# Row sums from one accumulated tensor, the normalisation on GpSimd, and matmul operands at one byte modulo 512

## The chip, the cores and the metric

The kernel runs on one core of a Trainium2 chip. A core has a matrix engine (TensorE, PE in the profile; its weight loads are listed apart as PEld), a vector engine (VectorE, DVE), a scalar engine (ScalarE, ACT), GpSimd (POOL), and a sync engine (SP) whose queue here issues nearly all transfers. Each engine works through its own instructions in the order in which they were written down and waits on semaphores for the others. Operands lie in on-chip memory (SBUF, 128 partitions), matmul results in eight banks of an accumulation memory (PSUM).

The metric is the device time of one execution in microseconds (us). A kernel is executed several times; one execution is also taken with the hardware profiler, and the profile's "span" runs from its first to its last instruction.

## What is computed

One transformer block on `x` of shape (2, 1024, 512) in float32: adaptive layer norm, causal attention with 32 query heads and 8 key/value heads of width 64, output projection with a gate, a second adaptive norm, and a feed-forward part with ternary weights. Cut to what matters here:

```python
q = apply_rope((x @ Wq).reshape(b, s, H, D).transpose(0, 2, 1, 3), pos)
k = apply_rope((x @ Wk).reshape(b, s, KVH, D).transpose(0, 2, 1, 3), pos)
v = (x @ Wv).reshape(b, s, KVH, D).transpose(0, 2, 1, 3)
scores = jnp.einsum('bhqd,bhkd->bhqk', q, k) / jnp.sqrt(jnp.float32(D))   # k, v repeated for 4 query heads each
scores = jnp.where(causal[None, None], scores, jnp.finfo(x.dtype).min)
attn = jax.nn.softmax(scores, axis=-1)
out = jnp.einsum('bhqk,bhkd->bhqd', attn, v)
x = x + ga * (out @ Wo)
h = _layernorm(x) * (1 + cb) + sb
gate, up = jnp.split(h @ ternary_quant(w_gate_up).T, 2, axis=-1)
x = x + gb * (rms_norm(silu(gate) * up) @ ternary_quant(w_proj).T)
```

The softmax's denominator is a sum over keys of the exponentials; the kernel computes it apart from the product with `v` and divides at the end.

## The kernel before

**Precision.** Most matmuls are F32R: each operand that needs more than that format holds is split into a high and a low part (names ending in H and L), and two or three products are added up in PSUM. A full F32R matmul has a 128x128 stationary tile and 512 moving columns. The product of exponentials and values (`po`) and the row sums (`pr`) are plain F32 matmuls, which the profile lists as two records each.

**Stages.** Four blocks of 512 tokens go through norm, transposes, keys (`pqk` from `wk`), values (`pv`) and queries (`pqk` from `wq`), with results stored to device memory. Then comes attention (some 300 to 1070 us), the output projection (`pj`, to some 1250 us), and the feed-forward part: hidden products (`pgu`, 16 chunks of 8+8 matmuls for each block of 512 tokens) and the second product (`pfo`, 8 matmuls for each chunk).

**Attention** is cut into 64 units (lines 576 and 755 on): batch, key/value head `g`, and 256 query positions `i`, for the four query heads of the group at once. A unit walks over `nb = 2*i + 2` blocks of 128 keys, so 2, 4, 6 or 8 of them; the last group walks `i` backwards. For each unit:
- `top_mm` and `top_red` (lines 797 and 805): high parts of queries and keys are multiplied to find each row's maximum (`pm`, reduced by VectorE into `mm` and `mx`), which is turned into a row and later subtracted from the scores by a fourth matmul (`unit` times `row`);
- `score(j)`: 4 pairs of matmuls into two PSUM banks, each pair on the two halves of the array's rows;
- `expo`: ScalarE writes the exponentials of key block j into the tile `e[j]` (128 keys x 4 heads x 256 queries); `causal`: GpSimd's affine_select blanks the upper triangle in the last two blocks;
- `value`: `po` accumulates values times `e[j]`, in steps of SPAN[nb] key blocks; `copy_out` copies it to `on`;
- `total(j, ...)` (line 901): the exponentials are added up into `acc`, half a tile (two heads) an instruction, the last block's in one. Before the change, all blocks but number nb-2 go into `acc`; the first add is `e[0] + e[1]`. VectorE does the adds of block j where `j % VSUM == 1` (with VSUM 9: block 1), and all adds of the last LAST units; GpSimd does the others (lines 942 and 943);
- `row_sum` (line 953): `pr = ones.T @ e[nb-2] + ones.T @ acc`, four matmuls of 256 columns each (one for each head, on a 32-column strip of the array), so eight; with nb = 2 it is `e[0]` and 128 columns of `e[1]`;
- `row_copy`, `row_turn`, `invert`, `put_inv`, `get_inv`: the sums go by three transfers through a narrow tile `l8` (where VectorE inverts them) and device memory (`linv`) and come back broadcast as `ri`; `normalize` (line 993) multiplies `on` by `ri` on VectorE; `keep` stores it.

**Order.** From line 587 on nothing is issued directly: every piece of work is a task with an engine, an estimated cost, a due time, the tasks it waits for and the buffers it takes, and `Plan.run` (line 102) writes them down one by one in the order that its own estimates give. TensorE's choice among ready tasks (line 131) goes by due time, less STICK for a task of the same array tiling as the one before, plus terms that favour tasks feeding VectorE (`feeds`: the maximum matmuls) when VectorE's backlog is under FEED, and disfavour them over ENOUGH. The array tilings are the modes: 0 full, 1 two column halves (`value`), 2 column strips (`row_sum`), 3 two row halves (`score`, `top_mm`). Once built, each engine's order is fixed.

**Buffers.** 6 + 10 tiles for exponentials (tags `e` and `eb`), 2 for `acc`, 4 for `on`, 2 for `ri`. An `e` tile is free again when its `value` and its adds (before the change, for block nb-2, the row sum) are done.

**Pools.** Tiles lie in pools opened and closed as the stages go. A pool starts where the one before it ends, so small tiles decide at which byte the large ones start. Before the change the small tiles `ct`, `st`, `mv`, `ve` and `rs` are in the first pool `lA`, beside the weights `wk` and `wv`, and `ve2`, `rs2` in the feed-forward pool `cC`. The build places the tiles so (start byte modulo 512): `wkH`, `wvH` 192; `wqH`, `hH`, `hL` 480; `t`, `k1`, `k2`, `h2_0`, `h2_1` 192; `vt` 192 and 480; `woH` and `woL` of the first four groups and `oh` 480, of the other groups 192; `gu0` to `gu5` 192, `gu6` onward 480; `mH`, `mL` and `pj0`, `pj1` 192, the other `pj` 320.

Nearly every instruction carries line 39, that of the recording helper, in the profile; tile names tell them apart.

Of the kernel before, what the change touches and what calls it, by code (L numbers as in the profile page):

```python
# [8 lines left out]
F32 = mybir.dt.float32  # L9
# [3 lines left out]
ALU = mybir.AluOpType  # L13
# [4 lines left out]
B, S, E = 2, 1024, 512  # L18
# [4 lines left out]
EC = E // 128  # L23
# [38 lines left out]
class Plan:  # L62
# [10 lines left out]
    def add(self, eng, cost, due, emit, after=(), order=(), takes=(), dma=0, mode=0, lane=None):  # L73
        t = Task(len(self.tasks), eng, cost, due, emit, after, order, takes, dma, int(isinstance(cost, Two)) if eng == "V" else mode, lane)
        self.tasks.append(t)
        return t
# [102 lines left out]
SPAN = {2: 2, 4: 4, 6: 6, 8: 4}  # L179
HELD = 4  # L180
TBEG, TEND, PER_UNIT = 300.0, 20.0, 0.8
VSUM, VSIGN, LAST = 9, 1, 3
TBEFORE, TGAP, TSKIP = 20, 20.0, 25.0
LEAD, SPREAD, STICK, LATE = 11.0, 0.6, 6.0, 2.0
ENTER, LEAVE, LOAD, AHEAD = 0.16, 0.37, 0.1, 0.25
CLASS = (0, 1, 1, 2)
TURN, SPARE = 0.05, 1.0
FEED, BOOST, ENOUGH, DELAY, FILL = 0.6, 12.0, 3.0, 8.0, 2.0
QT, PACE = 6, 4

@with_exitstack
def block_kernel(ctx, tc, x, wq, wk, wv, wo, wgu, wpj, cin, wmod, cos, sin, out):
    nc = tc.nc
    T = InOrder(tc, nc.tensor, True)
    V, A, P, SY = (InOrder(tc, e, False) for e in (nc.vector, nc.scalar, nc.gpsimd, nc.sync))
# [38 lines left out]
    ones = const.tile([128, 32], F32, name="ones")  # L234
# [73 lines left out]
    def pool(stack, name, bufs=1, **kw):  # L308
        return stack.enter_context(tc.tile_pool(name=name, bufs=bufs, reuse_waits="tile", **kw))


    left, right = ExitStack(), ExitStack()
    lp, hp0 = pool(left, "lA"), pool(left, "h0A")
    rp, hp1, tp = pool(right, "wA", side="right"), pool(right, "h1A", side="right"), pool(right, "tA", 2, side="right")

# [5 lines left out]
    cs = rp.tile([128, S], F32, name="cs")  # L321
    sn = rp.tile([128, S], F32, name="sn")

    ct = lp.tile([128, EC, B], F32, name="ct")
    SY.dma_start(ct, cin.rearrange("(k p) b -> p k b", p=128))
    A.activation(sc[:, :, 0:B], ct, AF.Silu)
    V.tensor_tensor(pick, ident[:, 0:B], ident[:, 32:32 + B], ALU.add)
# [64 lines left out]
    def stats(blk, t):  # L392
        d = st_x[blk]
        if t == 0:
            d["st"] = lp.tile([128, 4, 6], F32, name="st")
            d["mv"] = lp.tile([128, 4, 2], F32, name="mv", bufs=2)
        V.bn_stats(d["st"][:, t, :], d["x"][:, t, :])
        V.bn_aggr(d["mv"][:, t, :], d["st"][:, t, :])

    def rstd(blk, a=0, b=4):  # L400
        d = st_x[blk]
        if a == 0:
            d["ve"] = lp.tile([128, 4], F32, name="ve")
            d["rs"] = lp.tile([128, 4], F32, name="rs", bufs=2)
        V.tensor_scalar(d["ve"][:, a:b], d["mv"][:, a:b, 1], 1e-5, None, ALU.add)
        P.tensor_tensor(d["rs"][:, a:b], d["ve"][:, a:b], mhalf[:, a:b], ALU.pow)

# [158 lines left out]
    for blk in range(NT // 512):  # L566
        keys_values(blk)
        if blk < NT // 512 - 1:
            for g in range(KVH):
# [7 lines left out]
    NU = len(units)  # L577
# [11 lines left out]
                     h=2, h2=1, rab=2, rcd=2, rr=2, gs=2, hm=2, mH=2, mL=2, s2=2, sq=2, y=2, sm2=1))  # L589

    def pe(n):
        return n / 2400 + 0.018

    def dv(n):
        return 0.069 + n / 960

    def dd(n):
        return Two(dv(n))

    def po(n):  # L600
        return 0.2 + n * 0.00205
# [5 lines left out]
    add = plan.add  # L607
# [4 lines left out]
    for g in range(KVH):  # L612
        d, due = {}, 5.2 * g
# [121 lines left out]
    for u, (b, g, i) in enumerate(units):  # L735
        nb = 2 * i + 2
        for j in range(nb):
            due_s[(u, j)] = t
            n = 128 if j == nb - 1 else 256
# [12 lines left out]
    late_e = {key: n % (EB + EL) >= EB for n, key in enumerate((u, j) for u, (b, g, i) in enumerate(units) for j in range(2 * i + 2))}  # L752
    early = [key for key in late_e if not late_e[key]][:EB]

    def attention(u):
        b, g, i = units[u]
        d = U[u]
        nb = 2 * i + 2
        t0, t1_ = due_s[(u, 0)], due_s[(u, nb)]
        prev = U[u - 1] if u else None  # L760

# [7 lines left out]
        if u % NI == 0:  # L769
# [13 lines left out]
            for n in range(4):  # L783
                kd["l"].append(add("S", 0.46, t0 - 26 + n, lambda n=n: load_k(n), order=kd["l"] + (held or before),
                                   takes=(("k1",), (), ("k2",), ())[n], dma=256 * KB))
# [44 lines left out]
        for s in range(2):  # L830
            n = 2 * i + s + 1
# [4 lines left out]
        for n, (h0, s_, c, lo, hi) in enumerate(jobs):  # L836
# [3 lines left out]
            tag = "mx" if hi == 2 * i + s_ + 1 else "mm"  # L840
            for n_, h in enumerate((h0, h0 + 2)):
                r = add("V", dv(w) + ((0.075 if c else 0.015) if tag == "mx" else 0.0), due + 0.01 * n_, lambda a=(h, s_, c, lo, hi): top_red(*a), (m,), order=[low[h, s_]] if c else (),
                        takes=() if tag in seen else (tag,))
# [19 lines left out]
        def score(j):  # L863
            q0 = 128 if j == nb - 1 else 0
            for hp_ in range(2):
                d["p", j, hp_] = stile("ps_").rearrange("p (b q) -> p b q", q=256)
            for n in range(4):
                for hp_ in range(2):
                    r = slice(hp_ * 64, hp_ * 64 + 64)
                    w_, x_ = ((kd["k", 0], d["t"][r, 0]), (kd["k", 0], d["t"][r, 1]), (kd["k", 1], d["t"][r, 0]), (unit, rows[u % 2][r]))[n]  # L870
                    w_ = w_[r] if n == 3 else w_[r, j * 128:(j + 1) * 128]
                    T.matmul(d["p", j, hp_][:, :, q0:], w_, x_[:, :, q0:], start=(n == 0), stop=(n == 3))
# [35 lines left out]
        ex, es, vals, sums = {}, {}, [], []  # L908
        adds, later = {}, []
        for j in range(nb):  # L910
            n = 128 if j == nb - 1 else 256
            due = due_s[(u, j)]
            es[j] = []
            p = add("T", 4 * pe(2 * n) + 0.03, due, lambda j=j: score(j), d["lq"] + kd["l"] + [row] + (cleared[1:2] if u == 0 else []),
                    takes=("#", "#1"), mode=3)
            if late_e[u, j] or (u, j) not in early:
                p.order(opened)
            kd["use"].append(p)
            d.setdefault("sc", []).append(p)
            for hp_ in range(2):  # L920
                x_ = add("A", ac(2 * n), due + 0.5 + 0.5 * hp_, lambda j=j, h=hp_: expo(j, h), (p,), order=es[j],
                         takes=() if hp_ else ("eb",) if late_e[u, j] else ("e",))
                if late_e[u, j]:
                    x_.order(opened)
                p.hold(("#", "#1")[hp_], x_)
                es[j].append(x_)
            ex[j] = es[j]
            if j >= nb - 2:
                ex[j] = [add("P", 0.6, due - 1, lambda j=j: causal(j), es[j])]
            if (j + 1) % SPAN[nb] == 0:  # L930
                js = range(j + 1 - SPAN[nb], j + 1)
                v = add("T", (SPAN[nb] * 2048 - (1024 if j == nb - 1 else 0)) / 2400 + 0.02, due + 5,
                        lambda js=js: [value(x) for x in js], sum((ex[x] for x in js), []) + [kd["lv"]], order=vals[-1:],
                        takes=("#",) if j == SPAN[nb] - 1 else (), mode=1)
                kd["av"].append(v)
                vals.append(v)
            if nb > 2 and j > 0 and j != nb - 2:
                later.append((j, n, due))
        for j, n, due in later:
            for h in range(0, 4, 2 if n == 256 else 4):  # L940
# [8 lines left out]
        out_ = add("A", ac(512), due_s[(u, nb - 1)] + 5, copy_out, (vals[-1],), order=(opened,), takes=("on",))  # L949
# [2 lines left out]

        def row_sum():
            d["pr"] = xtile([128, 256], "pr")
            for n, (a, q0) in enumerate(((d["e", nb - 2], 0), (d["acc"], 0) if nb > 2 else (d["e", 1], 128))):
                for h in range(4):
                    T.matmul(d["pr"][h * 32:h * 32 + 32, q0:], ones, a[:, h, q0:], start=(n == 0), stop=(n == 1))

        def row_copy():
            d["ls"] = tp.tile([128, 256], F32, name="ls", bufs=1)  # L960
# [14 lines left out]
            for a in range(2):  # L975
                SY.dma_start(d["ri"][a * 64:a * 64 + 64, :], linv[u][a:a + 1, :].broadcast_to([64, 512]))

        rs = add("T", 8 * (256 if nb > 2 else 192) / 2400 + 0.02, t1_ + 4, row_sum, sums[-2:] + ex[nb - 2] + ex[nb - 1], takes=("#",), mode=2)
        d["rs"] = [rs]
        if sums:  # L980
            sums[0].hold("acc", rs)
        for j in range(nb):
            es[j][0].hold("eb" if late_e[u, j] else "e", vals[j // SPAN[nb]], *([rs] if nb == 2 or j == nb - 2 else adds[j or 1]))
        rc = add("A", ac(256), t1_ + 5, row_copy, (rs,), order=(opened,), takes=("ls",))
        rs.hold("#", rc)
        rt = add("S", 0.63, t1_ + 5, row_turn, (rc,), takes=("l8",), dma=16 * KB)
# [4 lines left out]
        gi = add("S", 0.92, t1_ + 8, get_inv, (pi,), takes=("ri",), dma=256 * KB)  # L991

        def normalize():
            V.tensor_tensor(d["on"], d["on"], d["ri"], ALU.mult)

        def keep():
            SY.dma_start(os_[b][g][:, :, i * 256:i * 256 + 256], d["on"].rearrange("p (a q) -> p a q", q=256))

        nm = add("V", dd(512), t1_ + 13, normalize, (gi, out_))
        gi.hold("ri", nm)  # L1000
        kp_ = add("S", 0.46, t1_ + 15, keep, (nm,), dma=256 * KB)
        out_.hold("on", kp_)
# [9 lines left out]
    for u in range(NU):  # L1012
        attention(u)
# [264 lines left out]
    n, count, before = 0, 4 * EC * 2 + FC, TBEFORE  # L1278
# [72 lines left out]
    def feed_forward(blk):  # L1351
        nonlocal prev_h, prev_p, prev_l
        d = Cd[blk]
# [47 lines left out]
        def proj(f, ts=range(4)):  # L1401
            if f == 0:
                d["po"] = [otile("pfo") for _ in range(4)]
            for t in ts:
                for n in range(2):
# [4 lines left out]
                  takes=(home_h(n),), dma=512 * KB) for n in range(2) for c in range(2)]  # L1410
# [4 lines left out]
        for f in range(FC):  # L1415
            if blk == 0:
                load_weights(f)
                if f >= PACE:
# [4 lines left out]
                      takes=("#", "gu")) for o in range(2)]  # L1423
# [24 lines left out]
            if final and f >= FC - 2:  # L1448
                p = [add("T", 2 * pe(512), due + 2 * STEP + 3.4 + 0.4 * t, lambda f=f, t=t: proj(f, (t,)), (mh, ml, lpj[f]), order=prev_p)
                     for t in range(4)]  # L1450
                for t in range(1, 4):
# [7 lines left out]
                    takes=("#", "#1", "#2", "#3", "po") if f == 0 else ())  # L1459
# [17 lines left out]
                T.matmul(d["pm"][:, t:t + 1], d["sq"][:, t * 128:(t + 1) * 128], ones[:, 0:1], start=True, stop=True)  # L1477

        def var2():
            d["ve"] = cp.tile([128, 4], F32, name="ve2", bufs=2)  # L1480
            V.tensor_scalar(d["ve"], d["pm"], 1.0 / HID, F32_EPS, ALU.mult, ALU.add)

        def root2():
            d["rs"] = cp.tile([128, 4], F32, name="rs2", bufs=2)
            P.tensor_tensor(d["rs"], d["ve"], mhalf, ALU.pow)

        def scale_y(t):
# [39 lines left out]
        for t in range(4):  # L1527
            cy.append(add("A", ac(512), due + 0.5 * t, lambda t=t: copy_y(t), (prj[-1],), order=cy[-1:] + list(gate_b_use),
                          takes=("y",) if t % 2 == 0 else ()))
# [51 lines left out]
```

## Time and profile before

| | |
|---|---|
| runs | 1624.47, 1624.91 and 1631.88 us; median 1624.91 |
| profiled execution | 1624.7 us |
| its span | 1622.0 us, 27506 instructions |
| mean granted TensorE clock | 0.994 of full |
| TensorE matmul busy | 1579.7 us, 97% of the span |
| VectorE busy | 1192.8 us, 74% |
| GpSimd busy | 763.3 us, 47% |
| ScalarE busy | 694.2 us, 43% |
| transfers | 239.58 MB, mean 148 GB/s |

A busy time is the union of an engine's instructions. Matmuls overlap in their pipeline, so a full F32R matmul lasts 390 to 400 ns by itself while one starts every 230 ns or so; the distance from start to start, or the length of a run of them divided by their number, is what counts. A row of the costliest groups names the tile written and the tiles read, the shapes, the number of instructions, busy time and mean length, and then the engine's idle time just before them with what ended most of it.

### The profile page before, as it was taken

The numbers are of one execution on the slowest core, as the hardware profiler recorded it, in microseconds if no ns is written. First come the engines' busy times: TensorE is split into PE (matmuls) and PEld (weight loads), VectorE is DVE, ScalarE is ACT, GpSimd is POOL, SyncE is SP. The second block draws the span as 40 slices with busy tenths as digits, with TensorE's granted clock in tenths as the row PEclk, the third lists the DMA queues.
The fourth block names the chain that finished last, engine by engine and source line by source line (L and its number), as shares of the span: only waits on it lengthen the run. The fifth ranks groups of instructions, "written<-read, shape, count | busy, mean of one in ns | idle before, by whom it ended". The sixth has DMA issues, their size and how long they took to land. (4 is left out here: it accounts for less than half of the span.)

```text
span 1622.0 us, 27506 instructions
## 1 busy us (share of the span) xinstructions
PE 1579.7 (97%) x9444; PEld 1098.8 (68%) x9444; DVE 1192.8 (74%) x2508; ACT 694.2 (43%) x1333; POOL 763.3 (47%) x678
## 2 busy tenths in 40 slices
PE   8999999999999999999999999999999999999998
PEld 7778887655655555555555555476777877888886
DVE  7888885888778778878898989857777674344434
ACT  4222122345546454554565566635555432222221
POOL 3445465455545545555545454603333544444343
PEclk9999999899999999999999999999999999999999
DMA  8774668565544453452554555386867733020000
GB/s 265 228 228 127 190 168 248 167 166 144 139 124 126 130 141 112 122 149 92 152 158 144 164 157 161 109 242 198 253 209 243 284 107 128 0 78 1 14 13 26
DMA packets 201219, 239.58 MB, mean 148 GB/s; under 512 B 33652, under 2 KB 142196, under 8 KB 201080
## 3 DMA queue, kind: packets, MB, share of 16 engines
q1 hardware_dynamic: 201080, 237.84, 49.1%
q8 instruction: 74, 1.21, 0.3%
q14 instruction: 65, 0.53, 0.1%
HBM read 148.90 MB, written 88.35 MB: 146 GB/s over the span
## 5 line engine op out<-in xcount | busy, mean ns | idle before, releaser
L39 POOL TENSOR_TENSOR acc<-acc,e 128x512 f32<-128x512 f32 x234 | 307.0, 1328 | 188.1 <-DVE acc L39 134.5
L39 PE MATMUL po<-e,vt 128*64 128x512 f32 (+1 forms) x1280 | 268.1, 561 | 3.9 <-DVE mx L39 2.0
L39 PE MATMUL pgu<-h,gu 128*128 128x512 f32 x1024 | 247.9, 395 | 0.0
L39 PEld LDWEIGHTS pgu<-h,gu 128*128 128x128 f32 x1024 | 192.3, 188 | 43.7
L39 DVE CUSTOM_DVE_ANT_0 junk<-pm,cmask,mm 128x384 bf16<-128x384 f32 (+1 forms) x256 | 174.5, 682 | 48.5 <-PE pm L39 27.1
L39 PEld LDWEIGHTS po<-e,vt 128*64 128x64 f32 x1280 | 85.6, 138 | 163.5 <-issue 138.5
L39 PE MATMUL pm<-k,t 64*128 64x384 f32 (+3 forms) x768 | 156.7, 366 | 9.8 <-DVE mx L39 7.6
L39 POOL TENSOR_SCALAR_AFFINE_SELECT e<-e 128x512 f32<-128x512 f32 x128 | 85.2, 679 | 160.9 <-ACT e L39 152.2
L39 DVE CUSTOM_DVE_ANT_0 junk<-pm,cmask 128x128 bf16<-128x128 f32 (+3 forms) x256 | 124.8, 488 | 44.0 <-PE pm L39 19.8
L39 DVE TENSOR_REDUCE mm<-pm 128x1 f32<-128x384 f32 (+2 forms) x256 | 130.0, 545 | 30.4 <-PE pm L39 29.3
L39 POOL TENSOR_TENSOR s<-hm 128x512 f32<-128x512 f32 x59 | 69.1, 1171 | 172.1 <-DVE hm L39 171.9
L39 PE MATMUL pj<-woH,oh 128*128 128x512 f32 x512 | 143.7, 402 | 0.0
L39 PEld LDWEIGHTS pm<-k,t 64*128 64x128 f32 x768 | 90.6, 184 | 65.6 <-DVE mx L39 21.6
L39 DVE TENSOR_TENSOR mL<-hm,mH 128x512 fp32r<-128x512 f32 x64 | 75.5, 1179 | 62.4 <-ACT mH L39 62.4
L39 DVE TENSOR_TENSOR hm<-gs,pgu 128x512 f32<-128x512 f32 x64 | 43.9, 686 | 102.5 <-PE pgu L39 100.2
L39 PEld LDWEIGHTS pj<-woH,oh 128*128 128x128 f32 x512 | 95.0, 189 | 21.1 <-issue 1.9
L39 ACT ACTIVATE mH<-hm 128x512 fp32r<-128x512 f32 x64 | 40.5, 633 | 149.2 <-PE pfo L39 139.4
L39 PE MATMUL pfo<-pj,mH 128*128 128x512 f32 x256 | 101.9, 398 | 0.0
L39 PE MATMUL pfo<-pj,mL 128*128 128x512 f32 x256 | 100.6, 393 | 0.0
L39 POOL TENSOR_TENSOR ra<-ra,rb 128x512 f32<-128x512 f32 x40 | 51.7, 1293 | 103.7 <-DVE rb L39 93.8
L39 ACT ACTIVATE on<-po 128x512 f32<-128x512 f32 x64 | 38.2, 597 | 141.6 <-PE po L39 138.7
L39 POOL TENSOR_TENSOR sq<-sq,s 128x512 f32<-128x512 f32 x59 | 80.7, 1367 | 4.5
(3556 smaller groups left out, 3809.8 us busy)
## 6 DMA issues: line engine op xcount, KB each, us to landing
qs<-rr SPq DMA_DIRECT2D x128, 256.0 KB
t<-qs SPq DMA_DIRECT2D x64, 512.0 KB
k<-ks SPq DMA_DIRECT2D x64, 256.0 KB
ri<-linv SPq DMA_DIRECT2D x128, 128.0 KB
os<-on SPq DMA_DIRECT2D x64, 256.0 KB
ks<-rr SPq DMA_DIRECT2D x32, 256.0 KB
w<-in_wgu SPq DMA_DIRECT2D x32, 256.0 KB
gus<-wr SPq DMA_DIRECT2D x32, 256.0 KB
```

The lines of the kernel that those rows point to most:

```text
L39: ins = f(*a, **k)
```

## The change

Four things change.

1. In units of more than two key blocks, except the last LAST, block nb-2 is added into `acc` as well (`whole`), and the row sum is one group of four matmuls over `acc`.
2. `normalize` is a GpSimd instruction.
3. The small tiles `ct`, `st`, `mv`, `ve`, `rs` and the feed-forward part's `ve2`, `rs2` move into a pool `sA`, opened before the others and kept to the end. With that, the build places all operands of F32R matmuls that belong together at byte 480 modulo 512. The F32 tiles `e` now lie at 192 and 416 (before: 416), `vt` at 224 and 480.
4. Constants of the planner: VSUM from 9 to 4, so that VectorE takes the adds of blocks 1 and 5; LAST from 3 to 4; STICK from 6 to 4; FEED from 0.6 to 1.0.

```diff
-VSUM, VSIGN, LAST = 9, 1, 3
+VSUM, VSIGN, LAST = 4, 1, 4
 TBEFORE, TGAP, TSKIP = 20, 20.0, 25.0
-LEAD, SPREAD, STICK, LATE = 11.0, 0.6, 6.0, 2.0
+LEAD, SPREAD, STICK, LATE = 11.0, 0.6, 4.0, 2.0
...
-FEED, BOOST, ENOUGH, DELAY, FILL = 0.6, 12.0, 3.0, 8.0, 2.0
+FEED, BOOST, ENOUGH, DELAY, FILL = 1.0, 12.0, 3.0, 8.0, 2.0
...
+    sa = pool(ctx, "sA")
     lp, hp0 = pool(left, "lA"), pool(left, "h0A")
...
-    ct = lp.tile([128, EC, B], F32, name="ct")
+    ct = sa.tile([128, EC, B], F32, name="ct")
...
-            d["st"] = lp.tile([128, 4, 6], F32, name="st")
-            d["mv"] = lp.tile([128, 4, 2], F32, name="mv", bufs=2)
+            d["st"] = sa.tile([128, 4, 6], F32, name="st")
+            d["mv"] = sa.tile([128, 4, 2], F32, name="mv", bufs=2)
...
+        whole = nb > 2 and u < NU - LAST
...
-            if nb > 2 and j > 0 and j != nb - 2:
+            if nb > 2 and j > 0 and (whole or j != nb - 2):
                 later.append((j, n, due))
...
-            for n, (a, q0) in enumerate(((d["e", nb - 2], 0), (d["acc"], 0) if nb > 2 else (d["e", 1], 128))):
+            parts = [(d["acc"], 0)] if whole else [(d["e", nb - 2], 0), (d["acc"], 0) if nb > 2 else (d["e", 1], 128)]
+            for n, (a, q0) in enumerate(parts):
                 for h in range(4):
-                    T.matmul(d["pr"][h * 32:h * 32 + 32, q0:], ones, a[:, h, q0:], start=(n == 0), stop=(n == 1))
+                    T.matmul(d["pr"][h * 32:h * 32 + 32, q0:], ones, a[:, h, q0:], start=(n == 0), stop=(n == len(parts) - 1))
...
-        rs = add("T", 8 * (256 if nb > 2 else 192) / 2400 + 0.02, ...
+        rs = add("T", (4 if whole else 8) * (256 if nb > 2 else 192) / 2400 + 0.02, ...
...
-            V.tensor_tensor(d["on"], d["on"], d["ri"], ALU.mult)
+            P.tensor_tensor(d["on"], d["on"], d["ri"], ALU.mult)
...
-        nm = add("V", dd(512), t1_ + 13, normalize, (gi, out_))
+        nm = add("P", po(512), t1_ + 13, normalize, (gi, out_))
...
-            d["ve"] = cp.tile([128, 4], F32, name="ve2", bufs=2)
+            d["ve"] = sa.tile([128, 4], F32, name="ve2", tag="mv", bufs=2)
...
-            d["rs"] = cp.tile([128, 4], F32, name="rs2", bufs=2)
+            d["rs"] = sa.tile([128, 4], F32, name="rs2", tag="rs", bufs=2)
```

The tile `e[nb-2]` of a whole unit is held until its adds are done instead of until the row sum is.

More of the change, by code (lines that the diff above doesn't have):

```diff
@@ L402, in rstd @@
         if a == 0:
-            d["ve"] = lp.tile([128, 4], F32, name="ve")
-            d["rs"] = lp.tile([128, 4], F32, name="rs", bufs=2)
+            d["ve"] = sa.tile([128, 4], F32, name="ve")
+            d["rs"] = sa.tile([128, 4], F32, name="rs", bufs=2)
         V.tensor_scalar(d["ve"][:, a:b], d["mv"][:, a:b, 1], 1e-5, None, ALU.add)
@@ L976, in get_inv @@
                 SY.dma_start(d["ri"][a * 64:a * 64 + 64, :], linv[u][a:a + 1, :].broadcast_to([64, 512]))
-        rs = add("T", 8 * (256 if nb > 2 else 192) / 2400 + 0.02, t1_ + 4, row_sum, sums[-2:] + ex[nb - 2] + ex[nb - 1], takes=("#",), mode=2)
+        rs = add("T", (4 if whole else 8) * (256 if nb > 2 else 192) / 2400 + 0.02, t1_ + 4, row_sum, sums[-2:] + ex[nb - 2] + ex[nb - 1], takes=("#",), mode=2)
         d["rs"] = [rs]
@@ L982, in attention @@
         for j in range(nb):
-            es[j][0].hold("eb" if late_e[u, j] else "e", vals[j // SPAN[nb]], *([rs] if nb == 2 or j == nb - 2 else adds[j or 1]))
+            es[j][0].hold("eb" if late_e[u, j] else "e", vals[j // SPAN[nb]], *([rs] if nb == 2 or j == nb - 2 and not whole else adds[j or 1]))
         rc = add("A", ac(256), t1_ + 5, row_copy, (rs,), order=(opened,), takes=("ls",))
```

## The prediction

> **What bounds the kernel now.** I read first the busy time of each engine by stage (windows of us; after the length: TensorE matmul, weight load, VectorE, ScalarE, GpSimd, then granted clock, DMA share, GB/s). The stages are first projections, attention, one stretch within attention, output projection, feed-forward.
>
> ```profile
> 0.00:300.00 300.00, 289.12 (x1338) 232.13 (x1339) 243.85 (x350) 77.89 (x127) 148.54 (x126) 0.99 0.70 207
> 300.00:1070.00 770.00, 749.08 (x5719) 434.37 (x5719) 631.87 (x1682) 417.38 (x853) 397.05 (x368) 0.99 0.49 141
> 840.00:1020.00 180.00, 171.71 (x1294) 96.69 (x1290) 161.73 (x414) 110.51 (x224) 91.13 (x86) 1.00 0.52 152
> 1070.00:1290.00 220.00, 215.78 (x967) 169.93 (x967) 159.17 (x296) 115.26 (x213) 71.02 (x68) 1.00 0.76 244
> 1290.00:1622.00 332.00, 325.72 (x1424) 262.35 (x1422) 157.91 (x182) 83.65 (x140) 146.66 (x117) 1.00 0.13 46
> ```
>
> TensorE covers 96 to 98% of every stage at full clock, so what shortens its stream shortens the kernel, as long as nobody else is as full. The one candidate is VectorE: 82% of attention, 90% (161.7 of 180) in its last part. GpSimd has room: 397 of 770, 52%.
>
> Next, the chain of work that ended last (start, length, what), once in attention and once in the feed-forward stage.
>
> ```profile
> 998.78 1.00 PE pr L39 x16
> ...
> 1053.08 0.79 PE pr L39 x16
> ```
>
> ```profile
> 1353.86 3.64 PE pgu L39 x16
> 1357.50 1.81 PE pfo L39 x8
> 1359.31 3.63 PE pgu L39 x16
> 1362.94 1.81 PE pfo L39 x8
> 1364.75 3.63 PE pgu L39 x16
> 1368.38 1.86 PE pfo L39 x8
> 1370.24 3.64 PE pgu L39 x16
> 1373.88 1.86 PE pfo L39 x8
> 1375.74 3.72 PE pgu L39 x16
> 1379.46 1.86 PE pfo L39 x8
> 1381.32 3.73 PE pgu L39 x16
> ```
>
> A row sum (`pr`) takes 1.00 us of TensorE. In units of two key blocks half of it runs over 128 columns instead of 256, and it takes 0.79: so 128 columns in four matmuls are 0.21 us, and a whole group of four is 0.42 to 0.43.
> In the second fence identical matmuls come in two speeds. A block's first six hidden chunks take 3.63 us for 16, later ones 3.72; its first two `pfo` steps 1.81 for 8, later ones 1.86. The steps fall where the tiles change pool: `gu0` to `gu5` start at byte 192 modulo 512 like the activations, `gu6` onward at 480; `pj0` and `pj1` at 192 like `mH` and `mL`, later `pj` at 320. The same byte for both operands: 227 ns each; different bytes: 233.
>
> Last, the costliest groups (busy us, mean ns, idle before).
>
> ```profile
> L39 POOL TENSOR_TENSOR acc<-acc,e 128x512 f32<-128x512 f32 x234 | 307.0, 1328 | 188.1 <-DVE acc L39 134.5 <-ACT e L39 19.4 <-DVE l L39 14.1
> ...
> L39 POOL TENSOR_SCALAR_AFFINE_SELECT e<-e 128x512 f32<-128x512 f32 x128 | 85.2, 679 | 160.9 <-ACT e L39 152.2 <-PE ps__3740 L39 4.3 <-DVE ws L39 3.8
> ...
> L39 DVE TENSOR_TENSOR acc<-e 128x512 f32<-128x512 f32 x96 | 82.2, 863 | 0.0
> ...
> L39 DVE TENSOR_TENSOR on<-on,ri 128x512 f32<-128x512 f32 x64 | 56.1, 878 | 2.0 <-DMA ri<-linv 1.9
> ```
>
> VectorE adds two such tiles in 863 ns, GpSimd in 1328. The normalisation waited for its inverse sums only 1.9 us in all 64 units.
>
> **Row sums.** `whole` holds for units of more than two blocks below number 60: 45 units. Each loses four matmuls (180 in all, and the changed program has 8022 for 8202). 45 x 0.43 = **-19.4 us** of TensorE. In exchange block nb-2 goes into `acc`: two adds for each of these units, 90 in all.
>
> **Who adds.** VSUM 4 gives VectorE the adds of block 5 too, and LAST 4 those of one more unit. By the two programs, GpSimd's adds go from 234 to 270 and VectorE's from 102 to 156. GpSimd: 36 x 1.328 = +48 us.
>
> **Normalising on GpSimd.** No row shows it; it is bounded by GpSimd's other two-input rows: 1.17 us (`s<-hm`) to 1.49 (`rc<-rc,rd`). I take 1.33 of the add, the same form: 64 x 1.33 = +85 us (75 to 95). GpSimd in attention becomes 397 + 48 + 85 = 530 of some 745, 71%. I cost it at nothing on the path: GpSimd now stands idle 152 us waiting for ScalarE's exponentials and 134 waiting for a VectorE add. If that cover fails, what is late is the causal mask queued behind, then the `po` matmul that reads it. VectorE loses 64 x 0.878 = 56 us and gains 54 x about 0.9 = 49, net -7. But its two-input operations stand aside for GpSimd's: `on<-on,ri` has a median of 686 ns against its mean of 878, a wait of 0.19. With GpSimd at 71 instead of 52% I scale that to 0.26, over 156 adds +11 us. VectorE's net is -7 to +4, nearly nothing.
>
> [...] The rows here give 1328 against 863, 1.5. [...]
>
> **Operand bytes.** By the two programs' placements, 1856 full F32R matmuls of 512 columns now have operands at different bytes: 640 `pgu`, 448 `pfo`, 384 `pj`, 192 for keys and 192 for values; after the change none has. Score and maximum matmuls agree already. 0.09/16 and 0.05/8 are 5.6 and 6.2 ns; I take 6: 1856 x 6 = **-11.1 us**, nearly all where TensorE alone sets the pace. [...]
>
> **Order.** STICK, FEED and the new costs shuffle attention. Changes of array tiling go from 264 to 273; a row sum keeps 1.00 - 2 x 0.43 = 0.14 for its two, so 9 x 0.07 = +0.6 us. Whether the new order waits more or less shows in no row; bounds: the 21 us that TensorE idles in attention now shrink by a third (-7) or grow by as much (+7). I take 0, as the waits named are short (`pm` on VectorE 20.4 us over 41).
>
> **Kept back.** In 180 of attention's 770 us VectorE is 90% busy and sets the pace with TensorE; that share of the row sums' gain, 19.4 x 0.23 = 4.5, I count as lost. The 384 early matmuls (2.3 us) lie where TensorE idles 10.9 us; half is lost, 1.1. Together **+5.6**.
>
> Sum: -19.4 - 11.1 + 0.6 + 5.6 = -24.3. The profiled execution took 1624.7 (its span of 1622.0 and 2.7 around it), 0.2 under the median of the runs: **1600 us**. Own range: 1588 (nothing kept back, idle -7) to 1611 (kept back twice over, idle +7 in part).
>
> **Rivals.**
> - *VectorE sets attention's length.* For: 90% in the last part, and GpSimd's contention grows. Against: over the whole stage it idles 138 us, 76 of it waiting for `pm` from TensorE. The row sums bring nothing, the bytes 10: 1615. Chance 0.10.
> - *The bytes are not the cause*, but something else that differs between those pools. Against: two tile pairs step at exactly the chunk where the byte changes. -19.4 + 0.6 + 4.5: 1610. Chance 0.07.
> - *More than that:* earlier feeding of VectorE removes two thirds of the idle time and nothing is kept back: 1624.7 - 30 - 14 = 1581. Chance 0.09.
> - *Slower: the normalisation blocks GpSimd's queue.* It waits there for a transfer chain (`linv<-l` 3.6 us and `ri<-linv` 2.8 in the chain of waits), and GpSimd runs in order; in the changed program 15 of 64 stand directly in front of a causal mask, the others in front of adds that later masks follow. If half the units show one whole 1.33 us on TensorE, 32 x 1.33 = 43: 1643. It decides from 24.3/64 = 0.38 us a unit. Against: VectorE, as in-order a queue, waited 1.9 us in all. Chance 0.10.
>
> **How the numbers follow.** The forecast has 0.64. This kernel's measurements tell about 0.5%, 8 us, from no change, so faster is below 1616.8: forecast 0.64, the bytes 0.07, more than that 0.09, and half of the VectorE case, 0.05: 0.85. Within 0.5%: the rest of that case and some of the slower one, 0.07. Slower: 0.08. The range 1586 to 1617 leaves out the slower case and most of the fastest.
>
> **What would show it.** `pr` x8 at about 0.57 us for 45 units; all `pgu` x16 at 3.63 and `pfo` x8 at 1.81; attention shorter by 14 to 20 us, everything after it by some 9; GpSimd at 70% of attention with `on<-on,ri` near 1.33 us. Wrong would be: TensorE waiting on GpSimd's `e` by more than today's 6.2 us, or VectorE above 90% with the stage unchanged.

## The result, and the profile after

The changed kernel took 1632.7 us (median of 11 runs, 1629.27 to 1637.75) beside 1625.64 for the kernel before: a ratio of 1.0044 [1.0027, 1.0061], about 7 us longer. That is inside the 0.5% named as telling nothing, though the interval leaves out 1; in any case the 25 us of gain are not there. The profiled execution took 1631.15 us, its span is 1629.4 at a mean clock of 0.993.

The windows by stage of the changed kernel (columns as in the prediction: TensorE matmul, weight load, VectorE, ScalarE, GpSimd, clock, DMA share, GB/s):

```profile
300.00:1070.00 770.00, 730.25 (x5283) 414.31 (x5281) 657.11 (x1660) 410.51 (x845) 529.77 (x465) 0.99 0.48 136
840.00:1020.00 180.00, 170.26 (x1248) 97.21 (x1246) 158.15 (x395) 99.25 (x204) 124.61 (x109) 1.00 0.47 132
1070.00:1290.00 220.00, 216.72 (x982) 171.19 (x983) 160.06 (x292) 114.16 (x211) 69.52 (x67) 1.00 0.76 240
1290.00:1629.00 339.00, 333.17 (x1484) 272.77 (x1482) 169.83 (x198) 89.47 (x150) 151.92 (x121) 1.00 0.17 59
```

In the window of attention TensorE's busy time fell from 749 to 730 of 770 us, but attention did not become shorter: TensorE now stands still for 40 us of the window instead of 21, and attention ends 16 us later. GpSimd reached 530 us, the very figure of the prediction; VectorE rose from 632 to 657, where it had been forecast to stay.

The tile `pj` of before, and then of after (duration in ns min/median/max, first and last start in us):

```profile
L39 PE MATMUL pj<-woH,oh x512: 387/395/587, 1053.8 to 1250.9; 128*128 128x512 f32 x171
```

```profile
L39 PE MATMUL pj<-woH,oh x512: 387/389/792, 1069.9 to 1264.8; 128*128 128x512 f32 x171
```

The output projection starts 16.1 us later. From its first to its last start it takes 194.9 instead of 197.1 us.

The chain of work that ended last, in the feed-forward stage of after (start, length, what):

```profile
1366.46 3.63 PE pgu L39 x16
1370.08 1.81 PE pfo L39 x8
...
1382.78 3.63 PE pgu L39 x16
1386.40 1.81 PE pfo L39 x8
...
1393.66 3.63 PE pgu L39 x16
```

All chunks now run at the fast speed. So the loss lies in attention alone. To see where, each matmul from 300 us on is counted from its start to the start of the next, without the time in which no matmul ran; that time has a line of its own (us, worked out from the traces' records):

| | before | after | difference |
|---|---|---|---|
| no matmul running | 25.1 | 43.0 | +17.9 |
| row sums `pr` | 60.9 | 41.7 | -19.2 |
| maxima `pm` | 108.9 | 121.7 | +12.8 |
| scores `ps` | 290.6 | 296.3 | +5.7 |
| values `po` | 262.5 | 259.6 | -2.9 |
| `pgu` and `pfo` | 357.4 | 351.0 | -6.4 |
| `pj` | 182.6 | 181.8 | -0.8 |

The sum is +7.1, of the span's +7.4. As TensorE's work the row sums gave what was forecast, and more than that went into standing still and into `pm` and `ps` that follow one another more slowly, which do exactly the same arithmetic as before.

Who made TensorE wait is in the waits of attention (300 to 1070 us), of before first (engine, instruction, what it waited for: us in all, times, longest):

```profile
PEld pm L39 <- DVE mx L39: 20.4, 41, 1.6
...
PEld pm L39 <- DVE mm L39: 7.4, 17, 0.8
...
PEld po L39 <- POOL e L39: 6.2, 17, 1.6
```

```profile
POOL on L39 <- DMA ri<-linv: 38.8, 24, 4.4
...
PEld pm L39 <- DVE mx L39: 25.2, 58, 1.1
...
PEld pm L39 <- DVE mm L39: 8.9, 25, 0.8
```

All rows in which TensorE or its weight load waits for VectorE, summed, go from 78.0 to 125.4 us; for GpSimd from 10.8 to 9.8, and for ScalarE from 28.5 to 23.7. (A matmul's row and its weight load's can cover the same time, so these sums rank the causes and are no loss of time.) GpSimd now stands before the transfer of `ri` for 38.8 us, yet TensorE waits no longer for GpSimd than it did. Of the engines that TensorE waits for, VectorE is the one that became later.

The costliest groups of after, by form:

```profile
L39 DVE TENSOR_TENSOR acc<-e 128x512 f32<-128x512 f32 x96 | 94.5, 990 | 5.4 <-ACT e L39 5.4
...
L39 POOL TENSOR_TENSOR on<-on,ri 128x512 f32<-128x512 f32 x64 | 84.9, 1327 | 78.2 <-DMA ri<-linv 73.5 <-DMA row<-mt 2.1 <-issue 1.8
...
L39 DVE TENSOR_TENSOR acc<-acc,e 128x512 f32<-128x512 f32 x60 | 57.1, 954 | 1.2 <-POOL acc L39 1.2
L39 DVE TENSOR_TENSOR wr<-ws,wsg 128x512 fp32r<-128x512 bf16 x48 | 48.2, 1004 | 0.7
```

The normalisation takes 1.327 us on GpSimd as forecast. But VectorE's adds went from 863 to 990 ns, and `wr`, which the change does not touch, from 842 to 1004.

### The profile page after: what moved, and what is told of

Its sections match the earlier page's. It is cut to its first block, busy times and chain, and to the rows that moved or that the text cites. A ratio compares the mean times of both kernels' runs of the same rounds, so it can differ in the third digit from the quotient of the medians.

```text
span 1629.4 us, 26894 instructions
## 1 busy us (share of the span) xinstructions
PE 1568.7 (96%) x9084; PEld 1091.1 (67%) x9084; DVE 1231.2 (76%) x2498; ACT 691.9 (42%) x1333; POOL 898.6 (55%) x778
## 5 line engine op out<-in xcount | busy, mean ns | idle before, releaser
L39 POOL TENSOR_TENSOR acc<-acc,e 128x512 f32<-128x512 f32 x270 | 361.2, 1352 | 90.7 <-DVE acc L39 62.8
L39 PE MATMUL po<-e,vt 128*64 128x512 f32 (+1 forms) x1280 | 264.6, 557 | 3.6 <-DVE mx L39 3.0
L39 PE MATMUL pgu<-h,gu 128*128 128x512 f32 x1024 | 244.0, 391 | 0.0
L39 DVE CUSTOM_DVE_ANT_0 junk<-pm,cmask,mm 128x384 bf16<-128x384 f32 (+1 forms) x256 | 174.3, 681 | 44.9 <-PE pm L39 22.1
L39 PE MATMUL pm<-k,t 64*128 64x384 f32 (+3 forms) x768 | 163.5, 372 | 18.3 <-DVE mx L39 6.4
L39 POOL TENSOR_TENSOR on<-on,ri 128x512 f32<-128x512 f32 x64 | 84.9, 1327 | 78.2 <-DMA ri<-linv 73.5
L39 DVE TENSOR_TENSOR mL<-hm,mH 128x512 fp32r<-128x512 f32 x64 | 76.8, 1200 | 60.7 <-ACT mH L39 60.7
```

What stands on the lines that cost most here:

```text
L39: ins = f(*a, **k)
```

## The experiments

All are variants of the kernel before or of the changed one. "Bytes" is the change's third part (the pool `sA`) alone. Ratios are to the kernel before, run on the same chip, with 95% intervals. A difference between two variants is worked out from their ratios, times 1626 us. "Idle" is the span less TensorE's busy time: 42.3 us before, 60.7 after.

### One part at a time

```diff
+    sa = pool(ctx, "sA")
-    ct = lp.tile([128, EC, B], F32, name="ct")
+    ct = sa.tile([128, EC, B], F32, name="ct")
```

(and the other small tiles of the change in the same way). Every engine has the same instructions in the same order as before; only addresses differ.

> The kernel before with the pool for small tiles alone; every engine's order is the same, instruction by instruction. If the start byte of the two operands is the cause of the two speeds: all full F32R matmuls start 227 ns apart, and the time falls by 9 us (1856 x 6 ns, less what the first stage hides), to about 1616. If something else in those pools is the cause: 1625, and two speeds remain.

To this, one part more: the `whole` lines; the normalisation on GpSimd; the four constants.

> Bytes and the fully accumulated row sums; normalisation on VectorE, the old constants. All 92 added adds go to GpSimd (some 120 us). Theory A (VectorE paces attention, and its two-input operations are held up by a busier GpSimd): the 19 us of TensorE are largely lost, 1608 to 1618, VectorE's adds of e take 0.95 us instead of 0.86. Theory B (the new constants made a worse order; the parts are sound): 1597, the full sum of both.

> Bytes and the normalisation on GpSimd; row sums as before, the old constants. VectorE gives up 56 us and pays for GpSimd's 85 with longer two-input operations. Theory A: 1616 to 1624, VectorE's busy time falls by no more than 30 us. Theory B: 1605 to 1612, since VectorE has 56 us less. A third theory (GpSimd stands in its queue for the inverse sums): 1625 or more, with GpSimd idle for ri and the masks late.

> Bytes and the new constants; row sums and normalisation as before. 54 adds go from GpSimd to VectorE, some 50 us. Theory A: VectorE is fuller, attention longer by some 15 us, 1625 to 1635, with VectorE over 85% of attention. Theory B: slower too, 1630 or more, but by waits of TensorE that do not go with VectorE's share. Should it be 1616 or less, the constants are harmless.

| | ratio | TensorE busy | idle | VectorE busy | GpSimd busy |
|---|---|---|---|---|---|
| before | 1 | 1579.7 | 42.3 | 1192.8 | 763.3 |
| bytes_only | 0.9945 [0.9933, 0.9958] | 1569.1 | 45.0 | 1196.3 | 763.0 |
| bytes_rowsum | 0.9981 [0.9969, 0.9993] | 1558.1 | 60.6 | 1218.7 | 886.9 |
| bytes_normpool | 0.9893 [0.9875, 0.9911] | 1566.0 | 38.5 | 1162.8 | 841.1 |
| bytes_constants | 1.0076 [1.0062, 1.0089] | 1587.6 | 48.8 | 1217.8 | 691.9 |
| after | 1.0044 [1.0027, 1.0061] | 1568.7 | 60.7 | 1231.2 | 898.6 |

The bytes are worth 9 us by the ratio, and 10.6 of TensorE's busy time. The normalisation on GpSimd is worth another 8.5, and not the nothing of the forecast. The row sums, meant to be the largest gain, cost 6 us, which neither theory had allowed: TensorE's busy time falls by 11.0 and its idle time rises by 15.6. The constants cost 21, with the same matmuls as bytes_only but 18.5 us more of TensorE's busy time.

Of these variants only bytes_only keeps the order. In every other one the planner writes a new order, so what a part is worth here includes what its new order is worth. How large that can be is shown further down, by variants in which nothing but the order differs.

### What eats the row sums' gain

The four-matmul row sum without the adds that feed it:

```diff
-            if nb > 2 and j > 0 and (whole or j != nb - 2):
+            if nb > 2 and j > 0 and j != nb - 2:
```

> Bytes, and the row sum of four matmuls over acc alone with no added adds: block nb-2 is left out of the denominators of 46 units. This takes 46 x 0.43 = 20 us from TensorE and adds nothing to anybody. If TensorE sets attention's length (the forecast's view): 1616.8 - 20 + 4.5 = 1601. If VectorE sets it: 1612 or more, TensorE's time between `pm` and score matmuls growing by what the row sums give up.

0.9876 [0.9853, 0.9899]: 11 us better than bytes_only. `pr` fell from 60.7 to 40.7 us, while the time without a running matmul rose from 27.2 to 37.7. So of 20 us of matmuls some 11 arrive even when nobody has to add anything more, and the adds (bytes_rowsum: time without a matmul 43.3, `pm` 114.0 where it was 107.5) take 17 more by the ratios.

Where they take it can be read from TensorE's progress. Attention has 4608 matmuls of `pm`, `ps` and `po`, by the profile's records. When the 4500th starts, 61 of `ps` and 48 of `po` are left in each of these kernels, with the records of `pr` that the table gives (us, worked out from the traces):

| | 4500th starts | `pr` left | first `pj` starts | between |
|---|---|---|---|---|
| before | 1034.5 | 64 | 1053.8 | 19.3 |
| bytes_only | 1033.8 | 64 | 1052.9 | 19.1 |
| short_rowsum | 1020.8 | 56 | 1040.8 | 20.0 |
| bytes_rowsum | 1017.3 | 64 | 1060.0 | 42.7 |
| after | 1047.8 | 64 | 1069.9 | 22.1 |

With the adds on GpSimd, bytes_rowsum is still 16.5 us ahead of bytes_only at this point, with the same work left. It then takes 42.7 us for what bytes_only does in 19.1, and ends attention 7 us behind. So the adds cost their time at the very end of attention, where GpSimd finishes them late. (The changed kernel is another case: it is 13 us behind the kernel before already at this point.) In short_rowsum attention ends 12 us earlier, and 7 of them are lost in the output projection, which takes 204.7 us to the first `pgu` where it took 197.3. The windows of bytes_only and of bytes_rowsum at the end of attention:

```profile
1020.00:1040.00 20.00, 19.99 (x144) 11.42 (x140) 14.54 (x35) 12.62 (x27) 11.09 (x10) 0.91 0.30 88
1040.00:1060.00 20.00, 19.27 (x135) 9.36 (x137) 15.92 (x24) 9.13 (x20) 6.79 (x6) 1.00 0.61 186
```

```profile
1020.00:1040.00 20.00, 14.48 (x75) 6.23 (x73) 8.57 (x10) 10.20 (x21) 13.94 (x14) 0.74 0.31 95
1040.00:1060.00 20.00, 8.37 (x63) 2.29 (x59) 16.00 (x23) 5.85 (x12) 12.41 (x10) 0.78 0.57 167
```

In bytes_rowsum TensorE stands still for 5.5 and 11.6 us of these two windows, and the granted clock (third figure from the end) drops to 0.74 and 0.78: the matmuls around the waits are slow as well (at a clock of 0.5 `pj` matmuls start 427 ns apart in the trace of after, for 227 at 1.0). The longest of these waits is of `pr` for GpSimd's `acc`:

```profile
PE pr L39 <- POOL acc L39: 6.2, 1, 6.2
```

The next longest, 3.8 us, is for ScalarE's `e`, and from 1000 to 1060 us ScalarE itself waits 5.2 us for GpSimd's `acc` before it writes `e`, for which it does not wait in bytes_only. The changed kernel with LAST 4 and VSUM 4 doesn't have this hole (22.1 us in the table).

With the normalisation on top, and the old constants:

> Bytes, row sums and normalisation on GpSimd with all old constants: GpSimd does all 92 added adds and the 64 multiplications (some +205 us, to 82% of attention). If the parts add up: 1607.5 + 4.6 = 1612, ratio 0.992. If VectorE's relief is what the row sums lacked: below 0.987. If GpSimd is now the bound: above 0.996, with TensorE waiting for masks.

1.0079 [1.0056, 1.0102]. The normalisation, worth -8.5 us alone, costs 16 here. GpSimd is busy for 78% of attention (583 of the 750 us from 300 to 1050). Again it is the end that is late: the 4500th matmul of the table above starts at 1027.2, 6.6 us ahead of bytes_only with the same work left, and the first `pj` at 1064.3, 11.4 behind. The matmuls' longest wait of the last part (1000 to 1070 us):

```profile
PE pr L39 <- POOL acc L39: 9.9, 1, 9.9
```

The second of the two windows there, and VectorE's add beside the fuller GpSimd (by form):

```profile
1040.00:1060.00 20.00, 10.43 (x54) 3.74 (x56) 6.91 (x9) 3.87 (x10) 16.76 (x17) 0.66 0.23 77
```

```profile
L39 DVE TENSOR_TENSOR acc<-e 128x512 f32<-128x512 f32 x96 | 103.8, 1095 | 0.7 <-ACT e L39 0.7
```

These two parts don't add up: what one is worth depends on which engine the other has filled.

### The constants, one by one

```diff
-VSUM, VSIGN, LAST = 9, 1, 3
+VSUM, VSIGN, LAST = 4, 1, 3
```

> Bytes and VSUM 4 alone: 47 adds go from GpSimd to VectorE (47 x 0.87 = 41 us), nothing else. If VectorE paces attention: 1628 to 1640, most of the 21 us that the constants cost. If the order that STICK and FEED make is the cause: 1617 to 1622.

```diff
-LEAD, SPREAD, STICK, LATE = 11.0, 0.6, 6.0, 2.0
+LEAD, SPREAD, STICK, LATE = 11.0, 0.6, 4.0, 2.0
-FEED, BOOST, ENOUGH, DELAY, FILL = 0.6, 12.0, 3.0, 8.0, 2.0
+FEED, BOOST, ENOUGH, DELAY, FILL = 1.0, 12.0, 3.0, 8.0, 2.0
```

> Bytes, STICK 4 and FEED 1.0 alone; who adds is unchanged. If VectorE's work is the cause of the constants' cost: within 4 us of 1616.8. If the order is: 1630 or more.

and each of these two lines by itself:

> Bytes and STICK 4 alone: TensorE changes its tiling 281 times instead of 264. If the changes of tiling are what STICK and FEED cost together: some half of it, 7 to 9 us over bytes alone (ratio to before near 1.000). If FEED is the cause: within 3 us of bytes alone (ratio 0.993 to 0.996).

> Bytes and FEED 1.0 alone: maximum matmuls are put ahead more often, 289 changes of tiling. If issuing them earlier only makes TensorE stand in its queue until VectorE has freed their banks: 8 to 16 us over bytes alone (ratio 1.000 to 1.004), with more TensorE waits for VectorE. If FEED is harmless: ratio 0.993 to 0.996.

Measured, all with bytes (alone 0.9945): VSUM 4 gives 0.9924 [0.99, 0.9948], no clear difference; STICK 4 gives 0.9905 [0.9883, 0.9928], 6.5 us better; FEED 1.0 gives 1.0033 [1.0019, 1.0047], 14 us worse; STICK and FEED together 1.0002 [0.9988, 1.0016]. FEED is the constant that hurts. With it no matmul running is 30.5 us instead of 27.2, `pm` takes 114.3 instead of 107.5, and `ps` 295.1 instead of 291.2. FEED decides below which backlog of VectorE, as the plan estimates it, TensorE takes a maximum's matmuls ahead of others; with 1.0 it does so sooner.

The same in the changed kernel, both constants put back, and FEED alone:

> The changed kernel with STICK 6 and FEED 0.6 put back; bytes, row sums, normalisation on GpSimd, VSUM 4 and LAST 4 stay. If the parts add up: some 17 us less than the changed kernel, ratio to before 0.985 to 0.993. If the old order suits only the old work: no faster than 0.998.

> The changed kernel with FEED 0.6 alone put back. If FEED is the part that loses and the others add up: 1632.7 - 14 = 1619, ratio 0.994 to 0.999. If the fuller GpSimd beside VectorE is what loses: 1.001 to 1.005, as with STICK and FEED put back.

With both old constants 1.0022 [1.0001, 1.0044]; with FEED 0.6 alone 0.9951 [0.9936, 0.9966], which is 15 us better than the changed kernel and faster than before. `pm` went from 121.7 to 116.3 us, `ps` from 296.3 to 292.5, the time without a matmul from 43.0 to 39.7. So FEED 1.0 costs 14 to 16 us in each of three pairs. The old STICK costs 11.5 us here, where it cost 6.5 beside the bytes alone. With FEED put back the changed kernel reaches the 4500th matmul of the table above at 1027.0 us, 7.5 ahead of the kernel before (72 records of `pr` are left, for 64), and its first `pj` at 1055.5, 1.7 behind. So it is some 9 us short at the end of attention once more, there with ScalarE's `e` as the longest wait.

What goes with FEED's cost shows in the waits. All rows in which TensorE or its weight load waits for VectorE, from 300 us to the first `pj`, summed as above:

| | FEED 0.6 | FEED 1.0 |
|---|---|---|
| bytes | 82.1 (bytes_only) | 112.0 (bytes_feed) |
| bytes, STICK 4 | 71.2 (bytes_stick) | 107.0 (bytes_stick_feed) |
| the changed kernel | 75.1 (after_feed06) | 125.4 (after) |

In each pair TensorE waits longer for VectorE with FEED 1.0.

### A theory that fell

VectorE's two-input instructions take longer than the plan believes (`acc<-e` 863 ns in before, for 0.60 us in the plan). If FEED 1.0 hurts because the plan takes VectorE for idler than it is, then true costs should repair it:

```diff
     def dd(n):
-        return Two(dv(n))
+        return Two(dv(n) + 0.27)
```

> Bytes and FEED 1.0, with the planner's estimate of a two-input VectorE operation raised by 0.27 us (0.60 to 0.87, the measured mean). If FEED hurts because the plan believes VectorE to be further than it is, and TensorE then stands before maximum matmuls whose banks are not free: most of the 14 us come back, ratio to before 0.993 to 0.998. If feeding early is costly as such (more changes of tiling, banks taken away from the scores): it stays at 1.001 to 1.005.

0.9909 [0.9884, 0.9933]: 20 us better than bytes_feed, as the theory wanted, and TensorE's waits for VectorE are back at 74.0 us. Then the two runs that could sink it, the same edit beside FEED 0.6, and in the changed kernel:

> Bytes with the planner's two-input VectorE estimate raised by 0.27 us, FEED 0.6. If the correction repairs FEED in particular: within 3 us of bytes alone, ratio 0.993 to 0.996. If it helps any order: 0.988 to 0.991.

> The changed kernel with the planner's two-input VectorE estimate raised by 0.27 us. If a plan too optimistic about VectorE is what turned the change into a loss: 14 us or more come back, ratio 0.990 to 0.997. If the fuller VectorE and GpSimd are the loss themselves: 1.000 or more.

0.9989 [0.9976, 1.0002], 7 us worse than bytes_only, and 1.018 [1.0163, 1.0196], 22 worse than the changed kernel. True costs don't make orders better in general; they make another order. With them FEED 1.0 is even the better choice by 13 us (0.9909 to 0.9989), at equal waits for VectorE (74.0 and 73.8 us). And in the changed kernel the edit brings the waits for VectorE down from 125.4 to 97.0 us while those for ScalarE go up from 23.7 to 56.1, so the waits for VectorE alone don't decide either. What is shown is that orders written down from slightly different estimates differ by -20 to +22 us with the same work. Which property of an order makes it good was not found.

### A version that beats both

The normalisation on GpSimd was the part that paid, so it was combined with the constant that paid, and with VectorE freed of its adds (VSUM 0 gives block 1's to GpSimd too):

```diff
-            V.tensor_tensor(d["on"], d["on"], d["ri"], ALU.mult)
+            P.tensor_tensor(d["on"], d["on"], d["ri"], ALU.mult)
...
-        nm = add("V", dd(512), t1_ + 13, normalize, (gi, out_))
+        nm = add("P", po(512), t1_ + 13, normalize, (gi, out_))
...
-VSUM, VSIGN, LAST = 9, 1, 3
+VSUM, VSIGN, LAST = 0, 1, 3
```

> Bytes, the normalisation on GpSimd, old row sums, and VSUM 0: GpSimd also does 92 of VectorE's 96 first adds (VectorE -80 us, GpSimd +122 to some 82% of attention). If VectorE's own busy time paces attention: below 1604, TensorE's waits for VectorE shorter still. If what counts is the hold-up between the two, or if GpSimd at 82% becomes the bound: 1608 or more, TensorE waiting for masks and acc from GpSimd.

> Bytes, normalisation on GpSimd and STICK 4; row sums, FEED, VSUM and LAST as before. If the gains add up: 0.9893 - 0.004 = 0.985, some 1601. If STICK's gain was a chance of its one order: 0.988 to 0.992.

> The same with VSUM 0, so that GpSimd also does the first adds. If VectorE's time is the bound: 0.981, some 1596, the fastest of all. If GpSimd at 80% of attention takes over: 0.985 or more.

0.9848 [0.9825, 0.9872], 0.9838 [0.9811, 0.9866] and 0.9843 [0.9816, 0.9869]: equal within their intervals. The windows of attention (300 to 1050 us) of bytes_only, then of normpool_vsum0:

```profile
300.00:1050.00 750.00, 727.04 (x5588) 418.98 (x5590) 623.08 (x1664) 411.27 (x841) 395.67 (x367) 0.99 0.48 138
```

```profile
300.00:1050.00 750.00, 737.38 (x5722) 434.12 (x5721) 535.02 (x1523) 415.08 (x851) 579.62 (x521) 0.99 0.50 144
```

VectorE falls from 623 to 535 us, GpSimd rises from 396 to 580 (77%), and TensorE gets 134 more matmuls through the same 750 us. The simplest of the three, the bytes, the normalisation on GpSimd and STICK 4 with everything else as before, has a median of 1605.68 us, on a chip on which the kernel before takes 1632.67. By the two ratios it is 2.05% under the changed kernel (0.9838/1.0044).

## Why the prediction was wrong, point by point

**Row sums, -19.4.** Right as TensorE's work: `pr` went from 60.9 to 41.7 us. What became of it was mis-sized. "Kept back" took 5.6 us as lost (4.5 of the row sums' 19.4), from the share of attention in which VectorE is some 90% busy. With no adds in exchange 9 of 20 us are lost already (short_rowsum), with the adds on GpSimd all of it and 6 more (bytes_rowsum); each number holds for its own order. The prediction reckoned with a loss where VectorE is full. In bytes_rowsum 16.5 us of the gain are there until 1017 us, and what took them is the end of attention: a late row sum waits 6.2 us for GpSimd's `acc`, TensorE stands still for 17.2 us between the 4500th matmul and the first `pj` (0.7 in bytes_only), and for 19.2 us there it has half its clock. The mean shares of 52% and 71% that the prediction looked at for GpSimd don't show this.

**Operand bytes, -11.1.** Right: 10.6 us of busy time and 9 us of time, from addresses alone (bytes_only, 0.9945 [0.9933, 0.9958]), with the steps between the chunks gone.

**Normalising on GpSimd.** The cost of one (1.33, measured 1.327), GpSimd's load (530 of 770) and the cover were right: TensorE's waits for GpSimd's `e` went down from 6.2 to 2.3 us. "Nothing on the path" was too cautious: beside the bytes, taking 56 us off VectorE is worth 8.5, its new order included. The rival of GpSimd's blocked queue was wrong in its place, the wait for `ri`: 73.5 us of it in the changed kernel, and no loss to see. GpSimd's queue does get late when the row sums' adds come on top (bytes_rowsum_normpool, 1638.45 us; the rival had said 1643), but through `acc` at the end of attention.

**VectorE's net, -7 to +4.** Wrong in size: VectorE's busy time rose by 38.4 us. By count the forecast holds, 56.1 us of normalisation less and 51.5 of adds more. The contention was scaled to 0.07 us over 156 adds, 11 us in all; measured, the other two-input instructions of VectorE became longer too, which the sum had left out. Before, by form:

```profile
L39 DVE TENSOR_TENSOR ws<-ws,wabs 128x512 bf16<-128x512 bf16 x96 | 49.6, 517 | 1.6
...
L39 DVE TENSOR_TENSOR wr<-ws,wsg 128x512 fp32r<-128x512 bf16 x48 | 40.4, 842 | 0.8
```

After, `wr` took 48.2 us and `ws` 57.4; with `ws<-ws,wm` and `wm` the four groups grew by 26, and `acc<-e` by 12. VectorE's instructions that read PSUM didn't: `junk` over 512 columns took 749 ns before and 748 after. The records show beside what the longer ones ran. In before the 51 of 96 `acc<-e` during which GpSimd ran nothing took 673 ns on average and 691 at most, the 28 that overlapped a two-input instruction of GpSimd 1240 on average; of `on<-on,ri` it was 685 (37) and 1289 (20). In after the same split gives 679 (30) and 1217 (54) for `acc<-e`, and 677 (15) and 1199 (30) for `wr`. `junk` over 512 columns took 747 to 749 ns in either case.

**Order, +0.6 and "0, bounds ±7".** This is the step that failed most. Of the 31 us between forecast and measurement it is 15: with FEED back at 0.6 the changed kernel is 8 us faster than before instead of 7 slower. The changes of array tiling were counted and priced, and the rest set to nothing because the waits named in the profile were short. FEED 1.0 alone costs 14 to 16 us beside the old cost estimates, beyond the bound and twice it, and TensorE's waits for VectorE grow by 30 to 50 us in the same pairs. The bound was a third of the time in which TensorE idles, and it missed that waiting can hide beside a matmul that still runs: the starts of `pm` and `ps` lie further apart, by 18.5 us in all that are not counted idle. The typical single matmul did not become longer (by shape, the median `pm` of 384 columns took 335 ns before and after, that of 512 columns 392 and 393). That these starts wait for VectorE to free a bank fits the waits of `pm` for `mx` and `mm`, but no run isolates it.

**The rivals.** "VectorE sets attention's length", at a chance of 0.10, named the engine for which TensorE waits longer in the changed kernel, and still forecast a gain (1615): it had the row sums bring nothing, while their adds and the order cost more than nothing. That a rebuilt order could lose by itself was no case of its own. The two signs of being wrong that the prediction named did not show either: the waits for GpSimd's `e` fell to 2.3 us, and VectorE is busy for 657 of 770 us, 85%.

**Still open.** Why one order of the same work is 20 us better than another, and why the parts don't add: one at a time, the four give -9 + 6 - 8.5 + 21 = +9.5, near the measured +7, but that is no proof of a sum. Some pairs add up (STICK with FEED, STICK with the normalisation, each within 3 us); row sums with the normalisation, on top of the bytes, should give -9 + 6 - 8.5 = -11.5 and gave +13. LAST was not tried alone. Whether an order without the late end would keep the 16 us that the row sums had gained until then was not tried either.

## What to carry to other kernels

When a planner writes the order, a change of its constants or costs is an edit with an effect of its own, here some 20 us in 1625 either way: run it apart from the edit that it comes with, and put its spread into the range. In this kernel it paid to take work off the engine that the busiest one waits for, though that engine was only 82% busy in the stage; work that left the busiest engine and landed on GpSimd brought nothing by itself, because it came late at the end of the stage. So look at the end of a stage too, and not only at its mean shares. Time each part alone and then in pairs, since a part's worth here changed its sign with the others.

## What the runs showed of the hardware

- Matmuls of 512 columns whose two F32R operands start at the same byte modulo 512 (both at 192, or both at 480) followed one another in 227 ns here; with one at 192 and the other at 480 or 320 it was 232 to 234. In the kernel before, by chunk and without the steps over 300 ns, `pgu` takes 227 to 230 ns in the first six chunks of a block and 233 to 234 in the other ten, `pfo` 227 to 228 in the first two and 232 to 233 in the others; in bytes_only all chunks take 227 to 230. Only addresses differ in bytes_only. Whether a smaller power of two than 512 would do, no run shows.
- VectorE's add of two SBUF tiles took 829 ns on average with GpSimd busy for 44% of the time from 300 to 1050 us (bytes_constants), 863 at 53% (before), 883 at 63% (bytes_normpool) and 1095 at 78% (bytes_rowsum_normpool). The share alone doesn't fix it: at 69% it was 920 in bytes_rowsum and 990 in after. GpSimd's own add hardly moved (1347 ns in bytes_constants, 1352 in after, 1342 in bytes_rowsum_normpool).
- In bytes_rowsum the waits of TensorE at the end of attention go with a lower clock that lasts beyond them. Its trace lists two stretches there at a granted clock of 0.5, of 10.2 and 13.7 us. They begin inside the waits of 3.8 and 6.2 us and last beyond them, 23.9 us in all; the kernel before has 3.4 there. What such a stretch does to matmuls shows in the trace of after: TensorE stands still for 2.8 us until 1068.9 us, the clock is 0.5 from 1068.7 to 1072.1, and in that time full `pj` matmuls start 427 ns apart, from 1072.4 on 227. What sets the length of a stretch was not shown.
